# First layer of a fused kernel: layer norm root on ScalarE, parts of the fronts and ends at other steps

## The chip, the core and the metric

The program runs on one core of a Trainium2 chip. The metric is the device time of one execution in microseconds. The core has TensorE (PE in the profile; PEld is its weight load), VectorE (DVE), ScalarE (ACT), GpSimd (POOL) and SyncE (SP, which here issues all the DMAs). Each engine works through its own queue in order; semaphores tie them together.

## The reference, cut to what matters

Two layers follow each other on x of shape (4, 384, 64, 64); the change is in the first, a selective state space (Mamba) block over the 4096 pixels of each image:

```
xs = group_norm(x) as tokens                       # (4, 4096, 384)
xn = (xs - mu) * rsqrt(var + 1e-5) * ln_w + ln_b   # layer norm over the 384 channels
xb, z = split(xn @ in_proj.T)                      # 768 each
xc = silu(causal_conv4(xb) + conv_b)
dt, Bm, Cm = split(xc @ x_proj.T)                  # 24, 16, 16
dt = softplus(dt @ dt_w.T + dt_b)
h  = exp(dt * A) * h + dt * xc * Bm                # 768 x 16 states, token by token
y  = (sum over states of h * Cm) + xc * D
x  = x + ((y * silu(z)) @ out_proj.T)
```

The second layer (an attention over 3x3 windows) is not touched.

## The kernel before, in words

**Chunks and steps.** The 4096 tokens of an image are cut into 17 chunks of 241 tokens (the last one of an image has 240), 68 chunks in all. The states of a chunk (768 channels x 16) are scanned in 12 *units* of 64 channels; the main loop (lines 776 to 824) does one unit in each *step* s, so a chunk takes 12 steps. Below, a step is named by its place in the chunk, 0 to 11. In step s, unit by unit: VectorE does `s_inputs2(s+1)` (half of dt*x*B into h, line 613) and two `s_scan(s)` (line 632); ScalarE does the carry and two times four decays `s_decay(s+1)` (exp(dt*A) into the PSUM tiles da, line 622), which need the scans of the same step to have freed da; GpSimd does `s_outputs(s-1)` (h times C, line 642) and `s_inputs(s+2)` (the other half of dt*x*B, line 598). In odd steps TensorE does `s_sum` (line 647), which adds the states of two units into the PSUM tile y. The tile h has five buffers (line 111), so the inputs of a later unit wait until `s_sum` has read an old one. The replicated dt and dt*x come back from DRAM by `s_fetch`, four steps ahead (line 779).

**Fronts and ends.** Around the scan, the dictionary `plan` (line 478) gives the place of each part of a chunk's *front*: load xt, mean (`f_mean`), centering (`f_center`), square, variance (`f_var`), root (`f_root`, `f_pow`), its broadcast by matmul (`f_rs`), `f_scale`, the projections `f_x` and `f_z` in three blocks each, the convolution `f_conv`, the SiLU, the small projection `f_bc` with `f_xd`, then dt (`f_dt`, `f_plog`, `f_dtx`, `f_log`), and the spread of B and C. The dictionary `ends` (line 513) does so for a finished chunk's *end*: load of the residual (`e_load`), output projection in three blocks (`e_project`) and `e_store`. A key (r, WHEN) is the step counted from the chunk's own position: r modulo 12 is the place in the chunk that is scanned at the time; a key of `ends` is 36 less than that count. WHEN is one of EARLY, READY, SCAN, POOL, MID, LATE (line 469), places within the step:

- EARLY, then `s_inputs2` and the gate, then READY, then scan, carry, first decay, save, second scan, SCAN, second decay, `s_outputs`, POOL, `s_inputs`, `s_sum`, MID, LATE.

Among parts of one place those of the later chunk come first (line 547). Every engine keeps this program order (class InOrder, line 34), so a part that stands at another place within the step changes an engine's queue only if that engine has something between the two places. For ScalarE there are thus two slots in a step: before the carry (POOL, MID, LATE of the step before, and EARLY, READY), and before the second decay (SCAN).

**PSUM.** All of the parts' matmuls share two buffers of one bank each, the tag "mm" (line 113): means, variances, projections, convolutions, dt, and the tile of `f_plog`. A matmul into one waits until the reader of the tile before it is done; which of the two a tile takes is chosen when the program is built. The tile of `f_plog` is read by `f_dtx` on VectorE, those of `e_project`, `f_x`, `f_z` and `f_conv` are copied out by ScalarE.

**The root.** `f_var` leaves 121 x 2 variances in PSUM; `f_root` adds 1e-5 on VectorE, `f_pow` raises to -0.5 on GpSimd (lines 292 to 299). ScalarE holds a table set with both logarithm and exponential (line 231), which is changed only around the SiLU (line 382).

Of the kernel before, what the change touches and what calls it, by code (L numbers as in the profile page):

```python
# [8 lines left out]
AF = mybir.ActivationFunctionType  # L9
ALU = mybir.AluOpType  # L10
# [39 lines left out]
def group_norm_coeffs(pe, ve, ae, gp, small, psum, blk12, mhalf, st, sc, bi):  # L50

    mv = small.tile([P, NCB, 2], F32, tag="mv", name="mv")
    neg = small.tile([P, 1], F32, tag="mg", name="neg")
    dev = small.tile([P, NCB], F32, tag="dev", name="dev")
    for cb in range(NCB):
        ve.bn_aggr(mv[:, cb, :], st[cb])
    yield False
    ps = psum.tile([P, 2, TM], F32, tag="mm", name="pm")  # L60
    for cb in range(NCB):
        pe.matmul(ps[:, 0, 0:1], blk12, mv[:, cb, 0:1], start=(cb == 0), stop=(cb == NCB - 1))
    yield True
    ae.mul(neg, ps[:, 0, 0:1], -1.0)
    ae.activation(dev, mv[:, :, 0], AF.Square, bias=neg)
    yield False
    ps = psum.tile([P, 2, TM], F32, tag="mm", name="pv")
    for cb in range(NCB):
        pe.matmul(ps[:, 0, 0:1], blk12, mv[:, cb, 1:2], start=(cb == 0), stop=False)
    for cb in range(NCB):  # L70
        pe.matmul(ps[:, 0, 0:1], blk12, dev[:, cb : cb + 1], start=False, stop=(cb == NCB - 1))
    yield True
    ve.tensor_scalar_add(sc, ps[:, 0, 0:1], 1e-5)
    gp.tensor_tensor(sc, sc, mhalf[:, 0:1], ALU.pow)
    yield False
    ae.mul(bi, neg, sc)
# [3 lines left out]
def mamba_layer(ctx, tc, x, w, x1, sc1, bi1, consts, behind):  # L80
# [16 lines left out]
    blk12, ident, eps, one = consts  # L97
    pe, ve, ae, gp, sp = (
        InOrder(tc, e) for e in (nc.tensor, nc.vector, nc.scalar, nc.gpsimd, nc.sync)
    )  # L100
# [22 lines left out]
    mhalf = wp.tile([P, 2], F32, tag="mhalf", name="mhalf")  # L123
# [168 lines left out]
    def f_root(c):  # L292
        n = c.spans[0][1]
        c.vs = front.tile([P, 2], F32, tag="vs", name="vs")
        ve.tensor_scalar_add(c.vs[:n, :], c.pv[:n, :, 0], 1e-5)

    def f_pow(c):
        n = c.spans[0][1]
        gp.tensor_tensor(c.vs[:n, :], c.vs[:n, :], mhalf[:n, :], ALU.pow)

    def f_rs(c):
        c.ps = pmm.tile([P, 2, TM], F32, tag="mm", name="ps_rs")
# [166 lines left out]
    EARLY, READY, SCAN, POOL, MID, LATE = range(6)  # L469

    def at(f, *args):
        def part(c):
            f(c, *args)

        part.f = f
        return part

    plan = {
        (-12, SCAN): [f_load],
        (-10, EARLY): [f_mean],  # L480
        (-10, READY): [f_center],
        (-9, POOL): [f_square],
        (-7, EARLY): [f_var],
        (-7, MID): [f_root],
        (-6, SCAN): [f_pow],
        (-5, READY): [f_rs],
        (-5, SCAN): [f_scale],
        (6, MID): [at(f_x, 0)],
        (8, EARLY): [at(f_z, 0)],
        (8, MID): [at(f_x, 1)],  # L490
        (9, POOL): [at(f_z, 1)],
        (9, MID): [at(f_conv, 0)],
        (10, LATE): [at(f_z, 2)],
        (11, LATE): [at(f_x, 2)],
        (12, SCAN): [at(f_conv, 1)],
        (12, LATE): [at(f_conv, 2)],
        (13, POOL): [at(f_silu, "xc", "zs")],
        (14, POOL): [f_bc],
        (15, EARLY): [f_xd],
        (16, READY): [at(f_dt, 0)],  # L500
        (16, SCAN): [at(f_dt, 1)],
        (17, EARLY): [at(f_dt, 2)],
        (17, READY): [at(f_plog, 0)],
        (17, MID): [at(f_dtx, 0)],
        (18, EARLY): [at(f_plog, 1)],
        (18, SCAN): [at(f_dtx, 1), at(f_plog, 2)],
        (19, READY): [at(f_dtx, 2)],
        (19, POOL): [f_log],
        (19, MID): [f_spread],
        (22, SCAN): [f_b],  # L510
    }

    ends = {
        (-9, READY): [lambda c: e_load(c)],
        (4, READY): [lambda c: e_project(c, 0)],
        (6, EARLY): [lambda c: e_project(c, 1)],
        (6, POOL): [lambda c: e_project(c, 2)],
        (15, EARLY): [lambda c: e_store(c)],
    }

    def chunk(k):
# [150 lines left out]
    def e_tokens(c, v):  # L672

        return v[c.b, :, c.t0 - 1 + c.lo : c.t0 - 1 + TM].rearrange("(p cb) l -> p cb l", cb=NCB)

    def e_load(c):
        c.lo = 1 if c.ci == 0 else 0
        c.xr = io.tile([P, NCB, XT], F32, tag="xr", name="xr")
        sp.dma_start(c.xr[:, :, c.lo : TM], e_tokens(c, x))

    def e_project(c, cb):
        lo = c.lo
        po = pmm.tile([P, 2, TM], F32, tag="mm", name="ps_out")
        pe.matmul(po[:, 0, lo:], ident, c.xr[:, cb, lo:TM], start=True, stop=False)
        for j in range(NJ):
            pe.matmul(po[:, 0, lo:], wout[:, j, cb, :], c.zs[:, j, lo:TM], start=False, stop=(j == NJ - 1))
        ae.copy(c.xr[:, cb, lo:TM], po[:, 0, lo:])

    def e_store(c):
        if c.ci == 0:  # L690
            st1[c.b] = small.tile([P, NCB, NC, 6], F32, tag="st1", name="st1")
        for cb in range(NCB):
            ve.bn_stats(st1[c.b][:, cb, c.ci, :], c.xr[:, cb, c.lo : TM])
        sp.dma_start(e_tokens(c, x1), c.xr[:, :, c.lo : TM])
        if c.ci == NC - 1:
            b = c.b
            st = [st1[b][:, cb].rearrange("p a s -> p (a s)") for cb in range(NCB)]
            made = group_norm_coeffs(
                pe, ve, ae, gp, small, pmm, blk12, mhalf, st, sc1[:, b : b + 1], bi1[:, b : b + 1]
            )  # L700
            norms.append([made, False])
# [18 lines left out]
    f_var(first)  # L720
    w_bias(2, 3)
    f_root(first)
    f_pow(first)
    f_rs(first)
    w_bias(3, NJ)
# [12 lines left out]
    f_conv(first, 0)  # L738
    f_var(second)
    f_root(second)  # L740
    f_pow(second)
    f_x(first, 2)
    f_rs(second)
# [14 lines left out]
    f_b(first)  # L758
    f_var(third)
    f_root(third)  # L760
    f_pow(third)
    for jj in range(NJ // 2):
        f_plog(first, jj)
# [12 lines left out]
    for s in range(-4, NU * (len(chunks) + 2)):  # L776
# [14 lines left out]
        if b + 1 < B:  # L791
            n, e = divmod(NU * ci + m - 3, NU // 2)
# [411 lines left out]
def layers(ctx, tc, w, out):  # L1204
# [26 lines left out]

    started = []
    mamba_layer(tc, x.rearrange("b c h w -> b c (h w)"), w, x1, sc1, bi1, consts, behind)
    outlook_layer(tc, x1, w, out, sc1, bi1, weights, ready)

# [65 lines left out]
```

## Time and profile before

| what | us |
|---|---|
| median of three runs | 6296.13 (6293.76 to 6303.95) |
| the profiled execution | 6290.02 |
| its span | 6288.2 |
| POOL: power of the root, 121x2, 68 times | 47.5 in all, 0.698 each |
| DVE: add before the root, 121x2, 68 times | 9.4 in all, 0.138 each |
| ACT: square of the front, 128x723, 68 times | 60.1 in all, 0.884 each |
| DVE scan, 128x968, 1632 times | 3452.7 in all, 2.159 each |
| POOL h times C, 128x1928, 816 times | 3228.3 in all, 3.956 each |
| ACT decay, 128x241, 6528 times | 3037.4 in all, 0.465 each |

In the profile's lines, out<-in are the program's tile names: da are the decays, h the states, y the sum over states, ps_in the x and z projections, ps_out the output projection, ps_dt, ps_lg and dtx the steps of dt, ps_ln the mean, vs the root. A number in brackets is idle time of the engine before the instruction and what ended it. All lines carry L45, the line of the helper that records the order.

### The profile page before, as it was taken

How to read it: one execution, taken by the hardware profiler on the slowest of the kernel's cores; microseconds unless marked ns; L12 is line 12 of the kernel's file. 1: busy time of each engine (PE TensorE's matmuls, PEld its weight loads, DVE VectorE, ACT ScalarE, POOL GpSimd, SP SyncE). 2: the span in 40 equal slices, each digit the busy share in tenths (PEclk: the TensorE clock that was granted, in tenths of full speed). 3: DMA queues.
4: the chain of work that ended last, by engine and by line, in shares of the span. 5: the costliest groups of instructions: out<-in, count | busy, mean ns of one | idle time of the engine just before them, and what ended most of it. 6: DMA issues, size and time to landing. Idle time of an engine off the chain costs nothing. (4 is left out here: it accounts for less than half of the span.)

```text
span 6288.2 us, 113395 instructions
## 1 busy us (share of the span) xinstructions
PE 5617.8 (89%) x40506; PEld 3964.7 (63%) x40506; DVE 5377.4 (86%) x4786; ACT 4986.7 (79%) x11842; POOL 5310.8 (84%) x2047
## 2 busy tenths in 40 slices
PE   6888888888888888888888888899888789999999
PEld 5666666666666666666666666666666455555555
DVE  4999999999999999999999999999999954454444
ACT  3888888888898888888889888888998844444544
POOL 3999999999999999999999999999999934333333
PEclk9999999999998999999999999999999899999999
DMA  4555555555555555545555545455554644445554
GB/s 128 133 135 147 150 130 134 132 137 140 145 134 139 138 132 142 141 129 142 138 140 148 134 125 137 127 135 140 130 132 129 174 140 165 166 164 171 170 169 145
DMA packets 640843, 894.22 MB, mean 142 GB/s; under 512 B 130249, under 2 KB 535163, under 8 KB 640148
## 3 DMA queue, kind: packets, MB, share of 16 engines
q1 hardware_dynamic: 640276, 886.96, 51.2%
q8 instruction: 319, 5.23, 0.3%
q14 instruction: 248, 2.03, 0.1%
HBM read 660.89 MB, written 225.70 MB: 141 GB/s over the span
## 5 line engine op out<-in xcount | busy, mean ns | idle before, releaser
L45 DVE TENSOR_TENSOR_SCAN h<-da,h 128x968 f32<-128x968 f32 x1632 | 3452.7, 2159 | 82.4 <-issue 57.4
L45 ACT ACTIVATE da<-dtr,aneg 128x241 f32<-128x241 f32 x6528 | 3037.4, 465 | 291.9 <-DVE h L45 129.2
L45 POOL TENSOR_TENSOR h<-h,bc 128x1928 f32<-128x1928 f32 x816 | 3228.3, 3956 | 12.1 <-DVE h L45 9.9
L45 POOL TENSOR_TENSOR h<-dxr,bc 128x964 f32<-128x964 f32 x816 | 1626.0, 1993 | 115.7 <-PE y L45 93.8
L45 PE MATMUL ps_in<-u,win 128*128 128x241 f32 x4896 | 1080.2, 374 | 82.1 <-DVE dtx L45 74.9
L45 PEld LDWEIGHTS ps_in<-u,win 128*128 128x128 f32 x4896 | 912.1, 191 | 247.8 <-DVE dtx L45 99.0
L45 POOL TENSOR_TENSOR bd<-ain,own 99x1188 f32<-99x1188 f32 x192 | 413.3, 2181 | 736.2 <-DMA ain<-ad 568.1
L45 DVE TENSOR_TENSOR h<-dxr,bp 128x964 f32<-128x964 f32 x816 | 931.6, 1142 | 109.1 <-PE y L45 96.3
L45 PE MATMUL y<-h,ssum 128*32 128x241 f32 x13056 | 907.6, 406 | 22.9 <-POOL h L45 21.8
L45 PEld LDWEIGHTS y<-h,ssum 128*32 128x32 f32 x13056 | 433.5, 119 | 438.7 <-issue 213.0
L45 PE MATMUL ps_cv<-xb,cdiag 128*128 128x241 f32 x3264 | 694.2, 368 | 5.3 <-ACT neg L45 4.2
L45 PEld LDWEIGHTS ps_cv<-xb,cdiag 128*128 128x128 f32 x3264 | 611.0, 189 | 78.4 <-issue 13.5
L45 PE MATMUL psv<-wv,xp 128*128 128x384 f32 x1728 | 591.2, 493 | 8.1 <-issue 7.7
L45 PE MATMUL ps_xd<-xc,wx 128*56 128x241 f32 x816 | 301.5, 549 | 321.0 <-ACT xc L45 321.0
L45 ACT ACTIVATE bd<-ain,own 99x324 f32<-99x324 f32 x704 | 335.3, 560 | 287.1 <-PE ps L45 275.9
L45 PE MATMUL ps_out<-zs,wout 128*128 128x241 f32 (+1 forms) x2448 | 540.0, 370 | 0.0
L45 PEld LDWEIGHTS ps_out<-zs,wout 128*128 128x128 f32 x2448 | 472.8, 193 | 38.0
L45 DVE TENSOR_TENSOR fold<-fold,ps 128x192 f32<-128x192 f32 (+1 forms) x768 | 211.4, 303 | 328.9 <-PE ps L45 314.6
L45 PEld LDWEIGHTS psv<-wv,xp 128*128 128x128 f32 x1728 | 321.4, 190 | 232.7 <-issue 16.9
L45 PEld LDWEIGHTS ps_xd<-xc,wx 128*56 128x56 f32 x816 | 152.7, 196 | 460.3 <-ACT xc L45 346.5
L45 PE MATMUL ps_dt<-xd,wdt 25*128 25x241 f32 x816 | 254.0, 437 | 117.6 <-ACT dt L45 81.0
L45 PE MATMUL y<-xc,ddiag 128*128 128x241 f32 x816 | 276.8, 424 | 10.0 <-DVE zs L45 10.0
(108 smaller groups left out, 5370.4 us busy)
## 6 DMA issues: line engine op xcount, KB each, us to landing
dxr<-dxd SPq DMA_DIRECT2D x1632, 120.5 KB
dtr<-dtd SPq DMA_DIRECT2D x1632, 120.5 KB
bc<-bcd SPq DMA_DIRECT2D x544, 120.5 KB
vin<-vd SPq DMA_DIRECT2D x384, 148.5 KB
vd<-vst SPq DMA_DIRECT2D x93, 576.0 KB
dxd<-dtx SPq DMA_DIRECT2D x272, 180.8 KB
dtd<-dt SPq DMA_DIRECT2D x272, 180.8 KB
xs<-in_x SPq DMA_DIRECT2D x96, 256.0 KB
```

What stands on the lines that cost most here:

```text
L45: return self.tc.keep_in_program_order(issue(*args, **kwargs))
```

## The change

The root is made on ScalarE in two instructions, the logarithm of variance + 1e-5 (the constant comes from the tile eps) and the exponential of -0.5 times that. Of `plan` and `ends` other places are given to a part of the entries; what the parts do stays the same. The group norm's own root (line 74) stays on GpSimd.

```
@@ f_root, f_pow
         c.vs = front.tile([P, 2], F32, tag="vs", name="vs")
-        ve.tensor_scalar_add(c.vs[:n, :], c.pv[:n, :, 0], 1e-5)
+        ae.activation(c.vs[:n, :], c.pv[:n, :, 0], AF.Ln, bias=eps[:n])
-        gp.tensor_tensor(c.vs[:n, :], c.vs[:n, :], mhalf[:n, :], ALU.pow)
+        ae.activation(c.vs[:n, :], c.vs[:n, :], AF.Exp, scale=-0.5)
@@ plan
         (-12, SCAN): [f_load],
-        (-10, EARLY): [f_mean],
-        (-10, READY): [f_center],
-        (-9, POOL): [f_square],
-        (-7, EARLY): [f_var],
-        (-7, MID): [f_root],
-        (-6, SCAN): [f_pow],
-        (-5, READY): [f_rs],
-        (-5, SCAN): [f_scale],
-        (6, MID): [at(f_x, 0)],
-        (8, EARLY): [at(f_z, 0)],
+        (-11, SCAN): [f_mean, f_center],
+        (-8, READY): [f_square],
+        (-8, MID): [f_var],
+        (-7, READY): [f_root],
+        (-6, READY): [f_pow],
+        (-5, SCAN): [f_rs, f_scale],
+        (7, READY): [at(f_x, 0)],
+        (8, SCAN): [at(f_z, 0)],
         (8, MID): [at(f_x, 1)],
-        (9, POOL): [at(f_z, 1)],
         (9, MID): [at(f_conv, 0)],
-        (10, LATE): [at(f_z, 2)],
-        (11, LATE): [at(f_x, 2)],
+        (10, READY): [at(f_z, 1)],
+        (10, MID): [at(f_x, 2)],
+        (11, MID): [at(f_z, 2)],
         (12, SCAN): [at(f_conv, 1)],
-        (12, LATE): [at(f_conv, 2)],
-        (13, POOL): [at(f_silu, "xc", "zs")],
-        (14, POOL): [f_bc],
+        (13, READY): [at(f_conv, 2)],
+        (13, MID): [at(f_silu, "xc", "zs")],
+        (14, READY): [f_bc],
         (15, EARLY): [f_xd],
         (16, READY): [at(f_dt, 0)],
         (16, SCAN): [at(f_dt, 1)],
         (17, EARLY): [at(f_dt, 2)],
         (17, READY): [at(f_plog, 0)],
-        (17, MID): [at(f_dtx, 0)],
-        (18, EARLY): [at(f_plog, 1)],
+        (17, MID): [at(f_dtx, 0), at(f_plog, 1)],
         (18, SCAN): [at(f_dtx, 1), at(f_plog, 2)],
         (19, READY): [at(f_dtx, 2)],
         (19, POOL): [f_log],
-        (19, MID): [f_spread],
+        (19, LATE): [f_spread],
         (22, SCAN): [f_b],
@@ ends
-        (-9, READY): [lambda c: e_load(c)],
-        (4, READY): [lambda c: e_project(c, 0)],
+        (-7, READY): [lambda c: e_load(c)],
+        (4, EARLY): [lambda c: e_project(c, 0)],
         (6, EARLY): [lambda c: e_project(c, 1)],
-        (6, POOL): [lambda c: e_project(c, 2)],
-        (15, EARLY): [lambda c: e_store(c)],
+        (6, SCAN): [lambda c: e_project(c, 2)],
+        (14, POOL): [lambda c: e_store(c)],
```

## The prediction

> **What bounds the kernel now.** I read the page's first two parts, then the waits, then the timeline of one chunk (a batch's 4096 tokens go in 17 chunks, 68 in all; a chunk is 12 steps, numbered 0 to 11 here), and then the same intervals over 64 chunks (all but the first two and last two). A chunk takes 72.25 us on average (start of scan to start of scan twelve steps later), so chunks fill about 5.0 ms of the span.
>
> ```profile
> span 6288.2 us, 113395 instructions
> PE 5617.8 (89%) x40506; PEld 3964.7 (63%) x40506; DVE 5377.4 (86%) x4786; ACT 4986.7 (79%) x11842; POOL 5310.8 (84%) x2047
> ```
>
> Between 116 and 4970 us the stage view has POOL busy 4740.18 of 4854 us (97.7%), DVE 4664.45 (96.1%). By busy share POOL would be the bound and the 0.69 us power on it a loss to recover. The waits say otherwise:
>
> ```profile
> DVE h L45 <- PE y L45: 96.3, 111, 6.4
> POOL h L45 <- PE y L45: 93.8, 91, 8.2
> PE ps_in L45 <- DVE dtx L45: 74.9, 66, 5.3
> DVE h L45 <- issue: 57.6, 51, 4.2
> ```
>
> Both engines wait for y: the sum over states (s_sum, on TensorE in odd steps), whose end frees an h buffer. "66" in the third line is once a chunk. Where these fall, in one chunk (start, duration, engine):
>
> ```profile
> 2041.42 1.97 PE L45 MATMUL ps_dt<-xd,wdt 25*128 25x241 f32 x4
> 2044.42 3.06 PE L45 MATMUL y<-h,ssum 128*32 128x241 f32 x32
> 2051.50 2.61 PE L45 MATMUL ps_out<-zs,wout 128*128 128x241 f32 x12
> 2055.39 2.72 PE L45 MATMUL ps_in<-u,win 128*128 128x241 f32 x12 [1.28 <-DVE dtx L45]
> 2058.89 1.84 PE L45 MATMUL y<-h,ssum 128*32 128x241 f32 x32
> ```
>
> ```profile
> 2047.53 1.16 DVE L45 TENSOR_TENSOR h<-dxr,bp 128x964 f32<-128x964 f32 x1 [1.16 <-PE y L45]
> 2053.06 0.63 DVE L45 TENSOR_TENSOR dtx<-ps_lg,xc 128x482 f32<-128x482 f32 x1
> 2054.68 0.66 DVE L45 TENSOR_TENSOR dtx<-ps_lg,xc 128x482 f32<-128x482 f32 x1
> 2060.76 1.16 DVE L45 TENSOR_TENSOR h<-dxr,bp 128x964 f32<-128x964 f32 x1 [0.42 <-PE y L45]
> ```
>
> ```profile
> 2049.61 0.69 POOL L45 TENSOR_TENSOR vs<-vs,mhalf 121x2 f32<-121x2 f32 x1
> 2060.90 1.98 POOL L45 TENSOR_TENSOR h<-dxr,bc 128x964 f32<-128x964 f32 x1 [0.86 <-PE y L45]
> ```
>
> ```profile
> 2053.73 0.67 ACT L45 ACTIVATE ps_lg<-dt,one 128x482 f32<-128x482 f32 x1 [0.53 <-DVE dtx L45]
> 2056.22 0.35 ACT L45 COPY xr<-ps_out 128x241 f32<-128x241 f32 x1
> ```
>
> Read them as a ring. The sum of step 5 ends (2047.48) and DVE starts 0.05 later; DVE's scans and dtx follow without a pause; TensorE's x projection (ps_in, 2055.39) starts 0.05 after the last dtx ends (2054.68 + 0.66), then rs, then the sum of step 7 (to 2060.73), and DVE starts at once. POOL waits 0.86 us at the end of the same stretch: its 0.69 us power lies inside this stretch and it still comes early. Over 64 chunks DVE waits for the sum of step 5 by 0.87 us (none to 2.0), for that of step 7 by 0.48, and at step 3 by 1.03 for ScalarE's decay after the SiLU; POOL waits 0.52 and 0.85 at steps 5 and 7, and the sums of these steps start 0.8 us or more after POOL delivered their h. So the ring is DVE, ScalarE, TensorE; POOL runs beside it.
>
> **The change, part by part** (per chunk, then times 66).
>
> 1. Power off POOL: 0.69 us, cover the 0.86 wait above. Worth 0; if POOL were the ring, 0.65 us (it overlaps its neighbour by 0.04) x 66 = 43 us gained. DVE's root add (0.14, net 0.05) stands just before the 1.16 us wait: 0.
>
> 2. Two ScalarE instructions of 121x2. No such row; the nearest are bi<-neg,sc 128x1 (295 ns, operand from a tile) and COPY st<-h 128x8 (188 ns). I take 0.29 each. The logarithm (step 5) delays the decays of unit 6, done 2.0 us (median; 1.5 in the lowest tenth) before their scan starts; the exponential (step 6) those of unit 7, done 1.6 or more before (second decay 1.05). Queued behind it are the carry and decays alone. Worth 0; uncovered, 0.58 x 66 = 38 us lost. No table load comes in: the logarithm of ps_lg and the exponential of da already alternate, and there are 137 loads, two a chunk.
>
> 3. Last output projection from after to before the step's second decay (6 POOL to 6 SCAN), and f_x of block 0 from 6 MID to 7 READY. For TensorE the order stays (project 1, project 2, x, rs, sum), but ScalarE's copy of project 2 (0.35) moves from 2056.22 to directly behind ps_lg (ends 2054.40), to 2054.75. Two PSUM buffers serve all these tiles; x now takes the one that the last dtx frees. If it takes the copied one instead, it starts at 2054.81, 0.58 sooner, and so does the sum. DVE can use only its 0.42 wait; where project 2 ends late (a tenth of chunks) the gain is 0.14. Minimum of the two over the chunks: 0.38 on average, x 66 = **25 us**. The copy before the second decay of unit 7 takes 0.36 of its 1.05 slack.
>
> 4. f_square to 4 READY, f_var to 4 MID, project 0 to 4 EARLY. ScalarE's slot before step 4 keeps its work (copy, square, exp: 1.6 us). TensorE does project 0 before, not after, the first dt, so that dt 1 and the variance start sooner. The last dt starts 0.05 us after the exp of dt 1 in most chunks, 0.69 in the worst tenth, 0.23 on average: 0.18 x 66 = **12 us** off the wait at step 5. From below, 0. Project 0 must end before ScalarE reaches its copy: sum of step 3 plus 3.3 us leaves 0.4 to 0.9.
>
> 5. f_mean and f_center to 1 SCAN. TensorE now does the mean (1.49) before the sum of step 1, and waits for the load xt in front of it.
>
> ```profile
> 2014.22 0.59 SPq L45 DMA_DIRECT2D xt<-in_x  x1
> 2019.45 1.49 PE L45 MATMUL ps_ln<-xt,avs 128*128 128x241 f32 x6
> 2030.80 2.17 DVE L45 TENSOR_TENSOR_SCAN h<-da,h 128x968 f32<-128x968 f32 x1 [0.77 <-issue]
> ```
>
> Counted from the first scan of step 0, the sixteenth semaphore update after the issue comes at 6.8 us (median; 6.0 and 7.7 in the outer tenths, 8.7 at worst); TensorE is ready for the mean at about 6.2 (conv ends at 5.4, plus 0.8 for what part 6 pushes later). Behind the mean in TensorE's queue is the sum (2.35), and DVE wants its buffer at 10.3 (s_inputs2 of step 2, after f_center). So the sum ends at 10.7 at the median, 0.4 late; DVE's own wait at step 3 (0.77 to 1.39) takes that up, since the SiLU that sets it doesn't hang on step 2. Chunk by chunk, what is left over is 0.14 x 66 = **9 us lost**; with TensorE or the load another 0.5 us later, 0.33 x 66 = 22; another 1.0, 0.63 x 66 = 41.
>
> 6. z and x of later blocks: z 0 to 8 SCAN, z 1 from before to after the sum of step 9, x 2 and z 2 exchanged. One projection is 2.6 us. The sum of step 9 starts sooner (POOL's h then limits it); that of step 11 has 2.9 us of TensorE more before it than POOL's delivery less 1.0 early start and 1.8 regained: still met, against DVE's slack of 1.8 or more. 0.
>
> 7. Orders that stay: conv 2 (0 LATE to 1 READY), SiLU, f_bc, plog 1, f_spread, e_store's statistics pass nothing on their engines. SP: e_store now comes before f_xd's two bcd writes, e_load two steps later, so that SP no longer waits for the store to land (189.5 us over 67 times). Loads run four steps ahead of their use: 0.
>
> 8. Start: the third front's root now stands in ScalarE's queue before the first plog, which started at 92.31 while the variance ended at 94.23. plog 0 and f_log come about 1 us later: **1 us lost**, with 5 us either way for the squeezed second chunk.
>
> Sum: 25 + 12 - 9 - 1 = 27 us off the profiled execution's 6290.02 us (span 6288.2), 6263. The median of the three runs, 6296.13, lies 6.1 above that execution, so I forecast 6269.
>
> [...] From 2040.10 to 2046.90 the granted clock was 0.50, and the sum of step 5 takes 4.07 us at the median against 2.35 at step 7; TensorE's longest pause in the 9 us before the sum's end is 1.09.
>
> [...]
>
> **Rivals.**
> - B, the buffer choice stays: x still waits for the last dtx. For: project 2's copy was already issued ahead of x in the program before, and x took the other buffer. Against: the copy was then later than dtx, now it is sooner. Part 3 is 0: 12 - 9 - 1 = 2 us, so 6294.
> - C, slower: the mean, held by the load in TensorE's queue, delays the sum of step 1 and with it DVE. It decides once the mean starts 0.9 us later than I have it (some 0.56 x 66 = 37 us lost, and the start's 1, against 37 gained). For: the load's issue and landing are fixed by SP's queue, and the mean now follows one step after. Against: DVE's 0.77 to 1.39 cover. At 1.5 us later, 1.06 x 66 = 70 us lost: 6290 + 70 + 1 - 37 = 6324, on the scale of the median 6330.
> - D, the clock: if project 0 before the dts keeps the clock up, the wait at step 5 goes as well: 0.87 x 66 = 57 in place of 12, so 6224.
> - E, POOL is the ring after all: 43 - 10 = 33, 6263; it can't be told from the forecast by time, only by POOL's waits.
>
> **How the numbers follow.** Forecast (with E) 0.54, B 0.18, C 0.2, D 0.08. The range must reach B and most of C and D: 6225 to 6320. Below 0.2% (12.6 us, about what a measurement can tell from no change) are 6283.5 to 6308.7: B whole, the edge of the forecast, a weak C. Faster 0.55 (most of the forecast, D), same 0.26, slower 0.19.
>
> **What would show it.** Right: DVE's wait for y at step 8 gone, ps_in following xr's copy instead of dtx, POOL's waits for y larger by about 0.7 us a chunk. Part 5: a wait of PE ps_ln for DMA xt of some 0.7 us a chunk and a smaller wait at step 3. Wrong: ps_in still behind dtx (B); new DVE waits for y at step 2 beyond 0.8 us (C); ACT da ending a scan's wait at steps 6 or 7 (part 2).

## The result and the profile after

| | median us | range, runs | ratio to before, 95% interval |
|---|---|---|---|
| before | 6288.81 | 6276.06 to 6303.95, 8 | |
| after | 6311.03 | 6302.29 to 6324.61, 8 | 1.0036 [1.0025, 1.0047] |

The change costs 0.36%, 22 us. It was forecast to gain 27: the sign is wrong. The time lies in the range only because the range was drawn wide enough to reach the slower rival C. The profiled execution of after took 6324.61 us (span 6322.8) and is the longest of its eight, 35 us above that of before (6290.02). So profiles tell *where* time goes below, and medians *how much*.

Intervals "per chunk" are means over the same 64 chunks as in the prediction. A chunk takes 72.89 us in after's profile and 72.25 in that of before, times 68 some 43 us. It is all in the chunks of the first layer: the stretch after them is 3 us shorter.

These are lines of after's waits (engine and tile that wait, what ends the wait: us in total, times, longest). They answer to the four of before:

```profile
POOL h L45 <- PE y L45: 185.4, 114, 8.1
DVE h L45 <- PE y L45: 157.9, 175, 6.3
PE ps_in L45 <- DVE dtx L45: 76.8, 63, 5.1
PE ps_ln L45 <- DMA xt<-in_x: 53.1, 36, 2.5
DVE h L45 <- issue: 28.8, 35, 3.9
```

POOL's power is gone and POOL waits twice as long for y (93.8 before). DVE's waits for y grew from 96.3 us in 111 pieces to 157.9 in 175: a new place has come in. The x projection still waits for dtx, as often and as long as before (74.9 us, 66 times). TensorE has a new wait, for the load xt. The row shows only a part of it: in 56 of 63 chunks TensorE stands for more than 0.1 us ahead of the mean, and in all of them the mean starts 0.135 us after the load has landed, so the wait is 87 us in all, 1.38 a chunk; the profile puts some of it down to ScalarE's tiles. "DVE h <- issue" (57.6 before) is the wait at step 3. By the step of the chunk, DVE's waits are:

| us a chunk | step 2 | step 3 | step 6 | step 8 | POOL, steps 5 and 7 |
|---|---|---|---|---|---|
| before | 0 | 1.03 | 0.86 | 0.48 | 0.52, 0.85 |
| after | 0.62 | 0.57 | 1.10 | 0.50 | 0.78, 1.72 |

The wait at step 2 is new and is only in part taken from step 3; that at step 6 grew by 0.24; the one at step 8, which the change was to remove, stands.

### The profile page after: what moved, and what is told of

Same layout as the page of the kernel before. It is cut to its first block, busy times and chain, and to the rows that moved or that the text cites. A ratio compares the mean times of both kernels' runs of the same rounds, so it can differ in the third digit from the quotient of the medians.

```text
span 6322.8 us, 113336 instructions
## 1 busy us (share of the span) xinstructions
PE 5638.1 (89%) x40506; PEld 3979.9 (63%) x40506; DVE 5376.9 (85%) x4718; ACT 5007.3 (79%) x11978; POOL 5263.7 (83%) x1979
## 5 line engine op out<-in xcount | busy, mean ns | idle before, releaser
L45 DVE TENSOR_TENSOR_SCAN h<-da,h 128x968 f32<-128x968 f32 x1632 | 3451.9, 2157 | 56.1 <-issue 28.8
L45 PE MATMUL ps_in<-u,win 128*128 128x241 f32 x4896 | 1094.2, 375 | 81.8 <-DVE dtx L45 76.8
L45 DVE TENSOR_TENSOR h<-dxr,bp 128x964 f32<-128x964 f32 x816 | 932.1, 1142 | 173.3 <-PE y L45 157.9
L45 PE MATMUL ps_xd<-xc,wx 128*56 128x241 f32 x816 | 278.6, 516 | 239.4 <-ACT xc L45 239.4
L45 PE MATMUL ps_dt<-xd,wdt 25*128 25x241 f32 x816 | 279.7, 476 | 113.9 <-ACT xr L45 71.9
L45 PE MATMUL y<-xc,ddiag 128*128 128x241 f32 x816 | 288.9, 440 | 10.2 <-DVE zs L45 10.2
```

The source lines that it names most:

```text
L45: return self.tc.keep_in_program_order(issue(*args, **kwargs))
```

## Experiments

All ratios are to runs of the kernel before that were taken alongside. "READY", "SCAN" and so on are the places in a step. The edits are given against the kernel named first.

### The root alone, and all but the root

Before, with the root as logarithm and exponential, at ScalarE's new places:

```
-        ve.tensor_scalar_add(c.vs[:n, :], c.pv[:n, :, 0], 1e-5)
+        ae.activation(c.vs[:n, :], c.pv[:n, :, 0], AF.Ln, bias=eps[:n])
-        gp.tensor_tensor(c.vs[:n, :], c.vs[:n, :], mhalf[:n, :], ALU.pow)
+        ae.activation(c.vs[:n, :], c.vs[:n, :], AF.Exp, scale=-0.5)
-        (-7, MID): [f_root],
-        (-6, SCAN): [f_pow],
+        (-7, READY): [f_root],
+        (-6, READY): [f_pow],
```

> The program before, with the root alone moved to ScalarE (logarithm at 5 READY, exponential at 6 READY). Theory M (the moved parts cost the time, the root nothing): within 6 us of the kernel before; POOL's wait at step 7 grows from 0.85 to about 1.5 us a chunk, DVE's waits stay at 0.86 (step 6) and 0.48 (step 8). Rival R (two more instructions on ScalarE hold up the decays): all or most of the 22 us loss. Rival P (POOL sets the pace): some 40 us faster.

Measured: 6289.44 us, ratio 0.9999 [0.9989, 1.0008].

After, with these four lines put back as they were before:

> The changed program with the root back on VectorE (5 MID) and GpSimd (6 SCAN). M: slower than before by the whole loss, 15 to 35 us; DVE's waits as in the changed program (0.6 at step 2, 0.6 at step 3, 1.1 at step 6). R: as before within 6 us. P: 60 us or more slower than before.

Measured: 6313.65 us, 1.0037 [1.0024, 1.005], the time of after.

So the root is worth nothing either way. POOL's own lines say why; first before, then the run with the root alone:

```profile
POOL h L45 <- PE y L45: 93.8, 91, 8.2
```

```profile
POOL h L45 <- PE y L45: 139.4, 103, 7.5
```

The power took 0.69 us a chunk, and 45.6 us of the 47.5 that it gave back are now spent waiting for y. Per chunk POOL waits 1.50 us in place of 0.85 at step 7, and nothing else moves (72.26 us against 72.25). An engine with 97.7% busy time in this stage was not the bound, which rules out rival E. On ScalarE the two instructions are short; these are groups of after (us in all, mean ns of one | idle before):

```profile
L45 ACT ACTIVATE vs<-ps_var,eps 121x2 f32<-121x2 f32 x68 | 17.4, 257 | 4.6 <-PE ps_var L45 4.6
L45 ACT ACTIVATE vs<-vs 121x2 f32<-121x2 f32 x68 | 14.1, 207 | 0.1
```

257 and 207 ns, where 290 each was estimated.

### The mean and the order of step 4, put back one at a time

After, with the mean at its old place:

```
-        (-11, SCAN): [f_mean, f_center],
+        (-10, EARLY): [f_mean],
+        (-10, READY): [f_center],
```

> The changed program with mean and centering back at 2 EARLY and 2 READY. M: DVE's wait at step 2 (0.62 us a chunk) goes, that at step 3 returns from 0.57 to about 1.03: net 0.16 us a chunk, 10 us faster than the changed program, if the step 5 part stays. Rival: the early mean also sets the clock of the next steps (TensorE's longer pause at step 1); then the wait at step 6 falls from 1.10 to 0.86 too and 25 us come back, all of the loss.

Measured: 6299.68 us, 1.0016 [1.0008, 1.0025].

After, with square, variance and project 0 at their old places:

```
-        (-8, READY): [f_square],
-        (-8, MID): [f_var],
+        (-9, POOL): [f_square],
+        (-7, EARLY): [f_var],
-        (4, EARLY): [lambda c: e_project(c, 0)],
+        (4, READY): [lambda c: e_project(c, 0)],
```

> The changed program with square, variance and the first output projection at their old places (3 POOL, 5 EARLY, 4 READY). M: DVE's wait at step 6 falls from 1.10 to 0.86 us a chunk, half clock at step 4 from 2.0 to 0.8 us a chunk: 16 us faster than the changed program. Rival (this order is not the cause of the later sum of step 5): wait at step 6 stays at 1.1, time as the changed program.

Measured: 6318.08 us, 1.004 [1.0026, 1.0054]: no gain.

After, with both put back:

> The changed program with mean and centering at 2 EARLY and 2 READY and with square, variance and first output projection at their old places. If these two groups carry the whole loss: within 6 us of the kernel before, DVE's waits 1.03 at step 3, 0.86 at step 6, 0.48 at step 8. Rival (the other moves, of x, z and the last output projection, cost something too): 8 to 12 us above the kernel before, as with the mean put back alone.

Measured: 6292.78 us, 0.9997 [0.9987, 1.0008]. The loss is in these two groups; all the other parts together are nothing within the interval. Which of square, variance and project 0 matters in the second group was not tried. But it isn't a sum: the old order of step 4 helps only where the mean is back as well. To see the mean by itself, before with the mean moved:

```
-        (-10, EARLY): [f_mean],
-        (-10, READY): [f_center],
+        (-11, SCAN): [f_mean, f_center],
```

> The program before with mean and centering alone moved to 1 SCAN. If the wait for the load costs what it does in the changed program: DVE's wait about 0.5 at step 2 and 0.7 at step 3, net 0.15 a chunk, 6300. Rival (with the old order of step 4 the late sum of step 1 costs more, as the mean's part did in the program with step 4 put back): 6310 to 6320.

Measured: 6316.05 us, 1.0033 [1.0019, 1.0047]: as large a loss as that of the whole change.

### Is it the mean's place, or its wait for xt?

SP issues the load of xt at step 0 behind eight DMAs of the fetches (from 2101.69 to 2107.04 us in one chunk of after, the load at 2107.09). Issued ahead of them it lands before TensorE wants it (in after with this edit TensorE's row of waits for xt is 1.1 us in one piece, in place of 53.1 in 36), and the mean's place stays:

```
-        (-12, SCAN): [f_load],
...
+        if m == 0 and 0 <= s and k + 3 < len(chunks):
+            f_load(chunk(k + 3))
         if m % 2 == 0 and unit(s + 4) is not None:
```

On after:

> The changed program with one more edit: the load xt is issued before, not after, the eight fetches of step 0, some 4 us sooner. If TensorE's wait for this load is what the early mean costs: the mean starts at about 5.5 us into step 0 instead of 7.2, DVE's wait at step 2 goes and the one at step 3 returns to 1.03; 10 us faster than the changed program, as with the mean put back. Rival (the mean's own 1.5 us on TensorE ahead of the sum is what costs): the wait at step 2 stays above 0.3 and the time within 5 us of the changed program.

Measured: 6298.94 us, 1.0015 [1.0006, 1.0024], the gain of the mean put back. On before with the mean moved:

> The kernel before with the mean and the centering two steps earlier, as in the run that moved them alone (6316, 1.0033), and the load of xt issued at the head of SP's queue in step 0, ahead of the fetches. Theory that the long chunks of that run come from TensorE's wait for xt: with xt there first, no wait of PE ps_ln for DMA xt, no chunk more than 2.5 us above the median, and the kernel before's time, 6288 to 6297 us. Rival, that the mean's new place in TensorE's order (not the wait) does it: still 6310 to 6320, with long chunks.

Measured: 6288.52 us, 0.9992 [0.9982, 1.0003]. On after with the old order of step 4:

> The changed kernel with the old order of step 4 (square, variance, project 0) and the early load of xt; the mean stays at its early place. Theory of two separate costs (the wait for xt about 11 us, the order of step 4 about 11 us): both are gone, 6287 to 6296 us, as with both places put back. Rival, that the mean's place costs without a wait: 6305 to 6318, as with the old order of step 4 alone.

Measured: 6290.66 us, 1.0 [0.999, 1.001]. The early mean is free once xt is there. The six ratios in one table:

| | old order of step 4 | new order of step 4 |
|---|---|---|
| mean at the old place | 0.9997 | 1.0016 |
| early mean, late load | 1.0040 | 1.0036 |
| early mean, early load | 1.0000 | 1.0015 |

Without the wait for xt the new order of step 4 costs 0.15 to 0.19% (9 to 12 us). The wait costs 0.40% (25 us) on the old order and 0.21% (13 us) on the new. So two costs make the loss, and they overlap.

How a wait costs is seen in one late chunk of the run with the mean alone. TensorE, then DVE (start, duration, engine, operation, in brackets idle time and what ended it):

```profile
718.55 1.85 PE L45 MATMUL ps_ln<-xt,avs 128*128 128x241 f32 x6 [2.62 <-DMA xt<-in_x]
720.19 1.01 PE L45 MATMUL y<-xc,ddiag 128*128 128x241 f32 x2
721.13 2.67 PE L45 MATMUL y<-h,ssum 128*32 128x241 f32 x32
```

```profile
720.44 0.97 DVE L45 SCALAR_TENSOR_TENSOR u<-xt,sc,ps_ln 128x723 f32<-128x723 f32 x1 [0.42 <-PE ps_ln L45]
723.85 1.16 DVE L45 TENSOR_TENSOR h<-dxr,bp 128x964 f32<-128x964 f32 x1 [2.44 <-PE y L45]
```

and three stretches of it (us, busy time by engine, granted clock of TensorE, share of the DMA engines, GB/s): the wait, mean and start of the sum, the rest of the sum:

```profile
715.00:718.50 3.50, 0.92 (x5) 0.52 (x3) 3.50 (x3) 3.40 (x10) 3.50 (x3) 1.00 0.92 231
718.50:721.80 3.30, 3.25 (x16) 2.24 (x20) 2.48 (x2) 3.10 (x9) 3.30 (x2) 0.65 0.55 151
721.80:724.80 3.00, 2.01 (x28) 0.83 (x20) 0.95 (x1) 2.97 (x4) 1.45 (x2) 0.82 0.00 0
```

The sequence is: TensorE stands 2.62 us behind the load, while the DMA engines are 92% busy. Then the granted clock is 0.50 for 3.4 us (8.9 to 12.3 us into the chunk), and the mean takes 1.85 us in place of 1.46 (48 of the run's 63 chunks) and the sum's matmuls against h 2.67 in place of 1.84. DVE waits 0.42 + 2.44 us at step 2, where the wait of step 3 can give back only 0.77 (its length in this chunk with the early load). From the mean's start to the end of the sum TensorE takes 5.25 us. With the early load, in a chunk of that run, it takes 3.55:

```profile
3185.80 1.38 PE L45 MATMUL ps_ln<-xt,avs 128*128 128x241 f32 x6
3187.01 0.57 PE L45 MATMUL y<-xc,ddiag 128*128 128x241 f32 x2
3187.51 1.84 PE L45 MATMUL y<-h,ssum 128*32 128x241 f32 x32
```

Over all chunks of the run with the mean alone, sorted by when the mean starts (us after the first scan of step 0), with DVE's waits, and how much longer the chunk is than the same chunk of before:

| mean starts | chunks | wait of TensorE | DVE at step 2 | at step 3 | later | longer, each | in all |
|---|---|---|---|---|---|---|---|
| before 6.5 | 19 | 0.65 | 0 | 1.02 | 1.05 | -0.31 | -6 |
| 6.5 to 7.0 | 12 | 1.16 | 0.15 | 0.72 | 1.27 | -0.54 | -6 |
| 7.0 to 7.4 | 14 | 1.66 | 0.78 | 0.36 | 1.49 | +0.38 | +5 |
| 7.4 to 8.0 | 16 | 1.90 | 1.70 | 0.27 | 2.64 | +2.48 | +40 |
| after 8.0 | 2 | 2.72 | 2.29 | 0 | 3.26 | +2.75 | +6 |

The eighteen chunks from 7.4 us on carry the whole loss: they are 45 us longer in the profiled execution, all 63 together 38. Up to 7.0 us the cover at step 3 holds; from 7.4 on little of it is left (0.27), and such a chunk loses more behind step 3 as well (2.64 against 1.05). The eighteen aren't alike. In eight of them half clock falls on the mean or the sum behind it, and these are 3.6 us longer each (28.8 in all); seven wait for xt as well but keep the full clock, 0.8 us each (5.4); and three, chunks 13, 30 and 47 counted from 0, start the mean late without any wait for xt (11.0). In after 26 chunks are this late, and are only 1.3 us longer each; why the new order of step 4 softens it isn't settled. With the early load the 12 chunks that were more than 2.5 us longer than in before become two; those two (13.7 us of half clock in steps 0 to 3) have no wait for xt; they are chunks 13 and 30 again, and what sets them off is open.

### What the x projection waits for

After, with x of block 0 behind the sum of step 7 in TensorE's queue, not ahead of it:

```
-        (7, READY): [at(f_x, 0)],
+        (7, MID): [at(f_x, 0)],
```

> The changed program with the first x projection behind the sum of step 7 (7 MID) instead of ahead of it (7 READY). If x, held by the last dtx through its PSUM buffer, sets the sum of step 7: DVE's wait at step 8 (0.50 a chunk) goes, POOL's at step 7 falls from 1.7 to below 1, and 0.5 x 66 = 33 us come off, 6278. Rival (the sum is set by something else, or the wait turns up at the next sum): 6311 within 8 us.

Measured: 6267.4 us, 0.9964 [0.9952, 0.9977]. The same line on after with mean and step 4 put back:

> Mean, square, variance and first output projection at their old places, and the first x projection behind the sum of step 7. If the x projection's 0.48 us wait at step 8 adds up with the rest: 6289 - 32 = 6257, DVE's waits 1.03 at step 3 and 0.9 at step 6 alone. Rival (POOL becomes the bound and its wait at step 5 the only one left): 6270 or more.

Measured: 6272.99 us, 0.9972 [0.9963, 0.9981]. So the wait of x for dtx is real and sits on DVE's path: the sum of step 7 stood behind x. (Here 6257 was expected if the wait at step 8 simply went; a rival expected 6270 or more with POOL as the bound. The time is the rival's, its reason isn't: the root back on POOL costs this program nothing, as the last section of experiments shows.) The change moved project 2's copy and not this order. In after, TensorE, DVE and ScalarE around it:

```profile
2365.91 2.61 PE L45 MATMUL ps_out<-zs,wout 128*128 128x241 f32 x12
2369.80 2.71 PE L45 MATMUL ps_in<-u,win 128*128 128x241 f32 x12 [1.29 <-DVE dtx L45]
```

```profile
2369.09 0.66 DVE L45 TENSOR_TENSOR dtx<-ps_lg,xc 128x482 f32<-128x482 f32 x1
2375.18 1.16 DVE L45 TENSOR_TENSOR h<-dxr,bp 128x964 f32<-128x964 f32 x1 [0.42 <-PE y L45]
```

```profile
2368.75 0.35 ACT L45 COPY xr<-ps_out 128x241 f32<-128x241 f32 x1
```

The copy out of project 2's buffer ends at 2369.10, and x starts only at 2369.80, 0.05 after the last dtx (2369.09 + 0.66). Over the 64 chunks the copy is done 0.70 us before x starts (median), and x starts 0.05 after dtx. The earlier copy didn't give x another buffer. With x behind the sum (lines of the last program below, which has the early load and the root on POOL as well):

```profile
2186.31 0.68 PE L45 MATMUL ps_rs<-ident,vs 121*128 121x121 f32 x4 [1.38 <-DVE dtx L45]
2186.82 0.58 PE L45 MATMUL y<-xc,ddiag 128*128 128x241 f32 x2
2187.33 1.84 PE L45 MATMUL y<-h,ssum 128*32 128x241 f32 x32
2189.10 5.16 PE L45 MATMUL ps_in<-u,win 128*128 128x241 f32 x24
```

```profile
2191.08 1.15 DVE L45 TENSOR_TENSOR h<-dxr,bp 128x964 f32<-128x964 f32 x1
```

Now rs takes the wait for dtx, the sum ends at 2189.17, and DVE's next h has no wait in front (0.42 to 0.50 before). Not all of it is won: at step 6 the wait grows from 0.90 to 1.26 us a chunk in the second of these runs. By the ratios the gain on after is larger (45 us) than on the other (16). On after the wait at step 6, already 1.10, grows by only 0.04. And its waits at steps 2 and 3 fall by 0.16 us a chunk together: the load of xt is issued 0.5 us sooner (in the median 1.45 in place of 1.99 us into the chunk), and 8 chunks in place of 26 have the mean after 7.4 us. That the one follows from the other isn't shown by itself.

### dt 2 and the variance elsewhere in step 5

If the thin matmuls ahead of the sum of step 5 are what it waits for, it should help to take one behind it. First the last dt, on after:

```
-        (17, EARLY): [at(f_dt, 2)],
...
-        (17, MID): [at(f_dtx, 0), at(f_plog, 1)],
+        (17, MID): [at(f_dt, 2), at(f_dtx, 0), at(f_plog, 1)],
```

> The changed program with the last dt projection behind the sum of step 5 (5 MID) instead of ahead of it (5 EARLY). If dt 2, which waits for ScalarE's exponential of dt 1, holds up the sum of step 5: that sum starts some 2 us sooner, DVE's wait at step 6 (1.10 a chunk) nearly goes, and 0.8 to 1.1 x 66 = 53 to 73 us come off. Rival (the wait turns up at dtx, x and the sum of step 7, which need dt 2): the wait at step 8 grows by as much, and the time stays within 10 us of 6311.

Measured: 6463.66 us, 1.0273 [1.0259, 1.0287]. Then the variance, on after with mean and step 4 put back and x behind the sum:

```
-        (-7, EARLY): [f_var],
-        (-7, READY): [f_root],
-        (-6, READY): [f_pow],
+        (-7, MID): [f_var],
+        (-6, READY): [f_root],
+        (-5, READY): [f_pow],
```

> As x_both with the variance behind the sum of step 5 (5 MID), root at 6 READY, power at 7 READY. If the sum of step 5 is held up by TensorE's line of dt 1, variance and dt 2: without the variance in it that sum starts sooner, DVE's wait at step 6 (0.9) falls to 0.3 or less, 40 us or more off x_both. Rival (ScalarE's exponential of dt 1, or the half clock, sets it and not the variance): wait at step 6 stays above 0.7, time within 10 us of x_both.

Measured: 6753.25 us, 1.0737 [1.072, 1.0755]. Both miss by far, and for one reason. Waits of the first, then of the second:

```profile
ACT xr L45 <- PE ps_out L45: 359.8, 136, 5.5
DVE dtx L45 <- ACT ps_lg L45: 230.2, 69, 8.9
PE ps_out L45 <- ACT dt L45: 150.5, 66, 3.9
```

```profile
ACT xr L45 <- PE ps_out L45: 617.5, 137, 9.9
DVE dtx L45 <- ACT ps_lg L45: 475.7, 69, 9.8
PE ps_out L45 <- DVE dtx L45: 466.7, 66, 7.5
```

The wait for y at step 6 is indeed gone in both: DVE's waits for y are 67.5 us in all in the first (157.9 in after) and 46.6 in the second (93.9 without the edit). But the tiles of dt, variance and projection share two PSUM buffers, and the order of the three engines is fixed: a late dt holds project 1 back until its exp is done, a late variance makes project 1 wait for dtx; ScalarE then stands in its queue for xr, and with it the ps_lg that dtx needs. DVE's wait of some 0.9 us at step 6 became one of 3.4 (230 / 68) and 7.0 us (476 / 68) ahead of dtx.

### The parts that hold, together

After, with mean and step 4 put back, x behind the sum, and the root on DVE and POOL again:

> As x_both with the root on VectorE (5 MID) and GpSimd (6 SCAN). If the ring still runs beside POOL: within 6 us of x_both. Rival (with the sum of step 7 no longer late, POOL's 0.65 us is on the path): up to 0.65 x 66 = 43 us slower than x_both.

Measured: 6266.6 us, 0.9963 [0.9949, 0.9978]. And the same with the early mean and the early load of xt:

> As the run before, with the x projection of block 0 at (7, MID), ahead of the sum's own turn in step 7, and the root on VectorE and GpSimd. Theory that the costs are separate and add: 6264 to 6273 us, as in the run with both places put back, x moved and the root on GpSimd (6267). Rival: the early mean still costs, 6275 to 6290 us.

Measured: 6267.6 us, 0.9955 [0.9942, 0.9967]. These two and the run of after with x behind the sum can't be told apart; all are about 0.4% faster than before and 0.7 to 0.8% faster than after.

## Why the prediction was wrong, point by point

**Parts 1 and 2 (root): right.** 0 (0.9999 with the root alone); POOL waits longer by what the power took.

**Part 3 (25 us): failed.** This is the larger term, and it fell by rival B's mechanism. The reading of the wait was right (x stands behind the last dtx, with DVE waiting for the sum behind it), and the copy did move where it was predicted: it starts 0.04 to 0.23 us after project 2 ends, 1.3 to 2.1 before. The step that failed is the inference that x would then take the buffer freed first. x starts 0.05 us after dtx in after as in before. The choice is made when the program is built, and no row of a profile can show it for an order that hasn't been built. The wait could be taken away by the order in TensorE's queue, which gave some 16 us on its own (0.9972 against 0.9997).

**Part 4 (12 us): the step worked, its sign didn't.** Variance and dt 1 do start sooner, and dt 2 does follow its exp more closely: with the mean put back 0.05 us on average, as predicted, against 0.23 in before (0.13 in after). But dt 2 then takes longer, 1.88 us on average in place of 1.59, and the sum of step 5 ends 0.17 to 0.22 later, not 0.18 sooner. The half clock of step 5 now begins earlier: at step 4 a chunk has 1.42 us of it with the mean back (2.02 in after), against 0.70 with the old order of step 4. The wait at step 6 grew from 0.90 to 1.07 us in that pair, 0.17 x 66 = 11 us; the ratios say 0.0019, 12 us.

The average hides two kinds of chunk. With the old order dt 2 takes over 1.9 us, at half clock, in 35 of 64 chunks, and DVE then waits 1.54 us for the sum; in 25 it takes some 1.08, and DVE waits only 0.07. With the new order 53 are of the first kind, with a wait of 1.14, and 2 of the second. So the gain that was forecast came in the slow chunks, 0.40 us each, and was more than lost on those that had been fast: the half clock that had set in behind the start of dt 2 now sets in ahead of it or with it.

One chunk that changed kind, with both parts put back, then with the mean alone put back:

```profile
2041.86 1.08 PE L45 MATMUL ps_dt<-xd,wdt 25*128 25x241 f32 x4 [0.37 <-ACT dt L45]
2043.86 3.08 PE L45 MATMUL y<-h,ssum 128*32 128x241 f32 x32
2046.98 1.16 DVE L45 TENSOR_TENSOR h<-dxr,bp 128x964 f32<-128x964 f32 x1
```

```profile
2047.71 1.97 PE L45 MATMUL ps_dt<-xd,wdt 25*128 25x241 f32 x4 [0.98 <-ACT dt L45]
2050.72 3.02 PE L45 MATMUL y<-h,ssum 128*32 128x241 f32 x32
2053.78 1.16 DVE L45 TENSOR_TENSOR h<-dxr,bp 128x964 f32<-128x964 f32 x1 [1.02 <-PE y L45]
```

The prediction took the wait at its average (0.87 us; in before 36 chunks had 1.45 and 25 had 0.02) and counted on the clock staying as it was. Rival D had the clock in view, but as a gain. That the earlier start of the thin matmuls *causes* the earlier half clock is argued from this order of events, not shown by itself.

**Part 5 (9 us lost): right mechanism, too small, and rival C's.** The landing was put at 6.8 us in the median; it came at 6.9. TensorE's wait for it was put at some 0.7 us a chunk and is 1.38. The cover at step 3 was there as well (0.57 left of 1.03). What failed is the price of a late load: the chunks were priced with the mean's and the sum's ordinary durations, and with nothing lost behind step 3. In the chunks where TensorE stands for 2.2 us or more (12 in the run with the mean alone) the mean takes 2.03 us on average in place of 1.46, the sum's matmuls can take longer too (1.7 us in all in the chunk shown), and more is lost behind step 3. So the tail counts, 18 of 63 chunks, and the term is 25 us in place of 9 on the old order of step 4 (13 on the new). The start from which rival C decides, 0.9 us later than forecast (7.8), was reached by seven chunks of that run and not by the median, 7.0. C's sign, a wait at step 2 beyond 0.8 us, shows only in the late chunks too; after's average is 0.62.

**Parts 6 and 7: 0, right**, as far as the run with mean and step 4 put back shows (0.9997), which keeps them. **Part 8:** the first two chunks came out 3 us shorter, not 1 longer.

Parts 3, 4 and 5 are thus the terms that failed. With the measured ones the sum is 0.16% for the order of step 4 (mean put back, against before) and 0.20% more for the early mean on it: 10 + 12 = 22 us lost, with nothing from part 3 against it, where 25 + 12 - 9 - 1 was forecast.

**The clock's row.** Part 4 took the clock as the profile of before has it: 0.50 from 2040.10 to 2046.90 us, with no pause of TensorE above 1.09 us in the 9 us before the sum's end. In the late chunk shown above the half clock follows a wait of 2.62 us. What sets it off isn't shown: of the late chunks that wait for xt, eight have it on the mean or on the sum behind it, and seven keep the full clock.

## What to carry to other kernels

Before crediting an earlier copy or reader with a freed buffer, look which buffer the next tile takes in the built order; if the wait matters, move the waiting instruction behind the one that matters. The mean's wait for its load (87 us in after) held up the sum queued behind it on TensorE, so price such a wait by the late tenth or quarter of the landings and not by the median, with the half clock that fell on the work behind it in eight of the late chunks here; issuing the load earlier took the wait away (1.0036 to 1.0015). A busy share of 97.7% is no proof of a bound: taking 0.7 us of work off POOL lengthened its wait by 0.65 us.

## What the runs showed of the hardware

- Of the 148 stretches at a granted clock of 0.50 in the run with the mean alone 82 lasted 3.4 us, 45 6.8, 17 10.2 and 3 13.7; of the 146 in before 74, 58, 11 and 1. Their total a chunk doesn't order the kernels by time: 10.5 us there, 10.6 in before, 12.3 in after with the early load, which is faster than the first (1.0015 against 1.0033), and 13.3 with mean and step 4 put back and x behind the sum, which is faster than before (0.9972).
- The four matmuls of the last dt (25 rows, 241 columns) took 1.08 us in the 22 of the 64 chunks of before that have them at a granted clock of 1.00 throughout, and 1.97 in the 35 that have them at 0.50 throughout.
- Where the mean waits for the load of xt, it starts 0.135 us after the sixteenth semaphore update of the transfer, in all 56 such chunks of after.
- Logarithm and exponential of 121x2 took 257 and 207 ns on ScalarE (mean of 68, after), the power 698 ns on POOL in before and 692 in the last program above.
